# Attention kernel: chunks turned by VectorE from rows loaded by quarters, norms alone through TensorE

## The chip, the cores and the metric

The kernel runs on one core of one Trainium2 chip. A core has a matrix engine (TensorE, in the profile PE, with its weight loads PEld), a vector engine (VectorE, DVE), a scalar engine (ScalarE, ACT), GpSimd (POOL) and a sync engine (SyncE, SP) that here only issues DMAs. The engines run their own instruction streams in order and wait for each other by semaphores. SBUF holds 128 partitions; TensorE writes to PSUM, of which the kernel uses eight banks of 128x512 floats. The metric is the device time of one execution in microseconds, the median over several runs.

## The reference

The input `x` is four images of 32 channels and 128x128 pixels. A first layer unfolds each image into 128 channels (c, r1, r2) of 64x64 pixels and lets the rows of the folded image attend to each other; a second layer runs on the tokens.

```python
def _L0_conv_ref(x, gamma):
    xs = x.reshape(B, C, h, R, w, R).transpose(0, 1, 3, 5, 2, 4).reshape(B, C * R * R, h, w)
    q = xs.reshape(B, C * R * R, hw)
    energy = jnp.einsum('bci,bcj->bij', q, q)
    d = jnp.sqrt(jnp.diagonal(energy, axis1=1, axis2=2))
    energy = energy / (d[:, :, None] * d[:, None, :])
    attn = jax.nn.softmax(energy, axis=-1)
    out = jnp.einsum('bcj,bij->bci', q, attn).reshape(B, C * R * R, h, w)
    out = gamma * out + xs
    ...
# second layer, t = tokens of x
t = t + attention without softmax(layernorm(t))
t = t + two experts of eight, by a router(layernorm(t))
```

Here `hw` is 4096 pixels, so `energy` is 4096x4096 for each image: every pixel's vector of 128 channels against every other's, divided by both norms.

## The kernel before

Everything is in float32. The 4096 pixels of an image are eight chunks of `CH` = 512 (`NCH` = 8), each of four blocks of 128 (`NJ`). Two forms of each chunk are needed: `qT`, pixels on partitions (the values, and the right side of the sums), and `qn`, channels on partitions, each pixel divided by its norm (both sides of the energy).

`attend(b, st)` runs the first layer for image `b`. For chunk `i` and every chunk `jc` up to `i` it takes four steps; in each a product `pe` (L556), its exponential `pr` by ScalarE (L559, with the row sums), and two steps later a product `po` with `qT` (L440). As the matrix is symmetric, the part above the diagonal is made from the part below: VectorE turns 32x32 blocks of `pr` into `F` (L369, L513), SP writes `F` to DRAM as `blocks` and brings it back as `G` (L483, L491), and some `LAG` = 57 units of a work clock later TensorE multiplies it into `pg` (L375), which VectorE adds to `o` (L385). `o` holds a chunk's sums as channels by pixels; ScalarE copies the first part into it from `po` (L445).

The second layer of image `b` (`layer1`: `close_rows`, `matrix`, `attention_rows`, `sorted_experts`) is a generator that is moved on between the steps of `attend` from 84% of image `b` on, and runs into image `b + 1`. `close_rows` divides the rows: `rdx` (1 over the sum, spread), its transposes `pbd` (L722), four multiplies `df` (L709) from PSUM, and an add into `T` (L731), the image's tokens.

`prep(b, kc, st)` prepares the pair `kc` of chunks (`2 kc` and `2 kc + 1`) and is the subject here. It loads `xx`, 128 partitions of (s, r1, c) with eight rows each, by four DMAs of 128 KB (L279). Image 0 loads all its `xx` into the buffer of `T`; the others have one buffer of the pool `xin`. TensorE transposes it in two groups of four (`ptq`, L313) and VectorE copies them out into `qT` (L302). VectorE squares `qT` and sums (L324, L325) and GpSimd takes the power -1/2 (L164). VectorE scales `qT` into `qs` (L338), TensorE transposes `qs` in two groups of four (`ptn`, L346) and ScalarE copies them into `qn` (L344). The transposes' banks come from `hold`, which keeps a PSUM bank of `ps_t` (three) until its copy is issued.

Below, a list `timed` gives each `prep` its begin and end in percent of an image's work and a count of moves; each move takes two of its steps (`yield`). Chunk pairs 0 and 1 of the next image are prepared at 65 to 82% and 87 to 99% of an image, pairs 2 and 3 at 2 to 20% and 30 to 50% of the image itself. `input_rows` loads the tokens `T` (for image 0 as 32 DMAs of 64 KB, for the others as 16 of 128 KB). The order in which the instructions stand on PE, DVE, ACT and SP is the order in which these generators issue them (`manual_schedule`).

## Time and profile before

| | |
|---|---|
| median of 3 runs | 1708.52 us (1704.93 to 1710.81) |
| the profiled execution | 1712.1 us |
| its span | 1710.3 us |
| granted TensorE clock, mean | 0.994 |
| DMA | 355.25 MB, 208 GB/s over the span |
| first matmul starts, last ends | 5.7 us, 1702.3 us |

The profile is of one execution. Its page lists the busy time of each engine, then the span in 40 slices with the busy share in tenths. The groups collect instructions of one line, engine and operation: out<-in, the shape, the count, then the busy time and the mean ns of one, then the idle time of the engine just before them and what ended it. The timeline has the start, the duration, and engine, line and operation; an `x2` on a matmul of 128x512 is one product, which the engine makes in two passes. The windows give the same by stretches of time.

## The change

The prepared chunks are made in another way, and the pixels of a chunk stand in another order inside its blocks.

- `load_quarters` loads a pair of chunks as `xa`: partition (a, c) holds rows 4a to 4a + 3 of the pair's half images, in four DMAs of 128 KB with runs of 2 KB. `xa` has the tag `xx` of the one-buffer pool `xin`.
- `turn_quarters` makes `qT` from it by VectorE's 32x32 transposes, two of 128x256 for each chunk. The pixels in a partition of `qT` stand in an order that follows from the quarters; `in_order` and `in_turn` bring `o` and the products into one another.
- Only 1 over the norms goes through TensorE: VectorE spreads `rn` into `wide`, four transposes give `pnorm`, and four multiplies of 64x512 make `qn` from the rows `xx` and `pnorm`. The rows are loaded too: for image 0 they are its tokens `T`, loaded once at the same time as `xa`, for the others `xx`, into the buffer that `xa` has left, after the transposes.
- The load of `xa` is issued five steps before its first transpose (two for pair 1 of image 0).
- The first pair of image 0 has a function of its own, `prep_first`, with `xa`, with `qs` and `ptn` as before, and with 40 spare transposes (`keep_running`) where 22 were.
- The places in `timed` are others: pairs 0 and 1 at 52 to 78% and 80 to 99%, pairs 2 and 3 at 1 to 22% and 28 to 52%; `input_rows` runs for images 1 to 3 alone.

```diff
-    def prep(b, kc, st):
...
+    def chunks_of(b, kc, st):
+        qT = qpool.tile([P, 2, NJ, P], F32, tag="qT", name=f"qT_{b}_{kc}")
+        st.setdefault("qT", {})[2 * kc] = qT[:, 0]
+        st["qT"][2 * kc + 1] = qT[:, 1]
+        return qT
+    def channels(b, kc, s, st):
+        qn = npool.tile([P, CH], F32, tag="qn", name=f"qn_{b}_{2 * kc + s}")
+        st.setdefault("qn", {})[2 * kc + s] = qn
+        return qn
+    def squares(b, kc, s, qT, ss):
+        sq = work.tile([P, NJ, P], F32, tag="qs", name=f"sq_{b}_{kc}_{s}", bufs=2)
+        nc.vector.tensor_tensor(sq, qT[:, s], qT[:, s], ALU.mult)
+        nc.vector.tensor_reduce(ss[:, ts(s, NJ)], sq, AX.X, ALU.add)
+    def rows_of_image(b, kc, st):
+        rows = st["T"][:, ts(kc, 8), :]
+        return rows.rearrange("p k (w r) -> p k w r", r=2)
+    def load_quarters(b, kc, queues=(nc.sync, nc.sync)):
+        xa = xin.tile([P, 2, 2, 2, HW2, 2], F32, tag="xx", name=f"xa_{b}_{kc}")
+        halves = x[b].rearrange("c (s g) w -> c s (g w)", s=2)
+        for a in (0, 2, 1, 3):
+            first_row = 16 * kc + 4 * a
+            queues[a // 2].dma_start(
+                xa[ts(a, S)].rearrange("p s k r w e -> p s (k r w e)"),
+                halves[:, :, first_row * W : (first_row + 4) * W],
+            )
+        return xa
+    def turn_quarters(s, xa, qT):
+        for k in range(2):
+            nc.vector.transpose(
+                qT[:, s, 2 * k : 2 * k + 2, :].rearrange("p h (e r c) -> p r (h e) c", e=2, r=2),
+                xa[:, s, k].rearrange("p r (h t) e -> p (r h) e t", h=2),
+            )
+    def prep_first(st):
+        b, kc = 0, 0
+        st["T"] = big1.tile([P, KT, D], F32, tag="T", name="T_0")
+        xa = load_quarters(b, kc, (nc.sync, nc.scalar))
+        qT = chunks_of(b, kc, st)
+        yield
+        ss = stat.tile([P, 2 * NJ], F32, tag="ss", name=f"ss_{b}_{kc}")
+        rn = stat.tile([P, 2 * NJ, 1], F32, tag="rn", name=f"rn_{b}_{kc}")
+        for s in range(2):
+            turn_quarters(s, xa, qT)
+            squares(b, kc, s, qT, ss)
+            pow_neg_half(rn[:, ts(s, NJ), 0], ss[:, ts(s, NJ)])
+        keep_running(40, ps_g, "pg")
+        scaled = []
+        for s in range(2):
+            qs = work.tile([P, NJ, P], F32, tag="qs", name=f"qs_{b}_{kc}_{s}", bufs=2)
+            nc.vector.tensor_tensor(qs, qT[:, s], rn[:, ts(s, NJ)].to_broadcast([P, NJ, P]), ALU.mult)
+            scaled.append(qs)
+        for s, qs in enumerate(scaled):
+            qn = channels(b, kc, s, st)
+            pt, done = hold(f"ptn_{b}_{kc}_{s}", lambda p, qn=qn: nc.scalar.activation(qn, p, AF.Copy))
+            for j in range(NJ):
+                nc.tensor.transpose(pt[:, ts(j, P)], qs[:, j, :], ident)
+            done()
+            yield
+    def prep(b, kc, st):
+        ahead = 2 if b == 0 and kc == 1 else 5
+        xa = load_quarters(b, kc)
+        if b == 0:
+            load_tokens(st["T"][:, ts(kc, 8), :], b, 8 * kc, 8)
+            xx = rows_of_image(b, kc, st)
+        for _ in range(ahead):
+            yield
+        qT = chunks_of(b, kc, st)
+        for s in range(2):
+            turn_quarters(s, xa, qT)
+            yield
+        if b > 0:
+            xx = xin.tile([P, 8, HW2, 2], F32, tag="xx", name=f"xx_{b}_{kc}")
+            load_tokens(xx.rearrange("p k w r -> p k (w r)"), b, 8 * kc, 8)
+        ss = stat.tile([P, 2 * NJ], F32, tag="ss", name=f"ss_{b}_{kc}")
+        def scale(s, spread, view):
+            qn = channels(b, kc, s, st)
+            own = slice(s * 64, s * 64 + 64)
+            for r2 in range(2):
+                nc.vector.tensor_tensor(
+                    qn[ts(r2, 64)].rearrange("p (j a t) -> p a j t", a=4, t=S),
+                    xx[own].rearrange("p (a k) (h t) r -> p r a (k h) t", a=4, h=2)[:, r2],
+                    view(spread[own]),
+                    ALU.mult,
+                )
+        rn = stat.tile([P, 2 * NJ, 1], F32, tag="rn", name=f"rn_{b}_{kc}")
+        for s in range(2):
+            squares(b, kc, s, qT, ss)
+            if s == 1:
+                pow_neg_half(rn[:, :, 0], ss)
+            yield
+        for _ in range(ahead - 2):
+            yield
+        wide = work.tile([P, NJ, 2, 64], F32, tag="qs", name=f"wide_{b}_{kc}", bufs=2)
+        for s in range(2):
+            nc.vector.tensor_copy(wide[:, :, s], rn[:, ts(s, NJ)].to_broadcast([P, NJ, 64]))
+        yield
+        def scale_all(bank):
+            for s in range(2):
+                scale(s, bank, lambda ap: ap.rearrange("p (j a t) -> p a j t", a=4, t=S))
+        bank, done = hold(f"pnorm_{b}_{kc}", scale_all)
+        for j in range(NJ):
+            nc.tensor.transpose(bank[:, ts(j, P)], wide[:, j].rearrange("p s c -> p (s c)"), ident)
+        yield
+        done()
+        yield
@@ -367,6 +417,12 @@
         queued[:] = [q for q in queued if q[0] > tick[0]]
         for f in due:
             f()
+
+    def in_order(ap):
+        return ap.rearrange("p (a j c) -> p j a c", a=4, c=S)
+
+    def in_turn(ap):
+        return ap.rearrange("p (j a c) -> p j a c", a=4, c=S)
     def transposed_share(b, st, i, jc, G):
@@ -381,8 +437,7 @@
                 junk, G[:, :, ib], AF.Copy, accum_out=st["sums"][:, NJ * i + ib, jc : jc + 1]
             )
             if ib == NJ - 1:
-                o = st["o"][jc].rearrange("p (j a c) -> p a j c", a=4, c=S)
-                nc.vector.tensor_tensor(o, o, pg.rearrange("p (a j c) -> p a j c", a=4, c=S), ALU.add)
+                nc.vector.tensor_tensor(st["o"][jc], st["o"][jc], pg, ALU.add)
                 st["got"][jc] += 1
             yield "done" if ib == NJ - 1 else None
@@ -401,7 +456,7 @@
                     junk[:, :, : ib * S], rows, AF.Copy, accum_out=st["sums"][:, NJ * i + ib, NCH:]
                 )
             if step == (2, 1):
-                o = st["o"][i].rearrange("p (j a c) -> p a j c", a=4, c=S)[:, :, :3]
+                o = st["o"][i].rearrange("p (a j c) -> p a j c", a=4, c=S)[:, :, :3]
                 nc.vector.tensor_tensor(
                     o, o, pg[:, : 3 * P].rearrange("p (a j c) -> p a j c", a=4, c=S), ALU.add
                 )
@@ -442,7 +497,7 @@
                 )
                 if row["left"] == 0:
                     o = opool.tile([P, CH], F32, tag="o", name=f"o_{b}_{i}")
-                    nc.scalar.activation(o, row["po"], AF.Copy)
+                    nc.scalar.activation(in_order(o), in_turn(row["po"]), AF.Copy)
                     st["o"].append(o)
             def below(tiles, blks, i=i, values=values):
@@ -521,7 +576,8 @@
                     row["back"] = psum_t(f"back_{b}_{jc}")
                 nc.tensor.matmul(row["back"], qT[i][:, j, :], w, start=(j == 0), stop=(j == NJ - 1))
                 if j == NJ - 1:
-                    nc.vector.tensor_tensor(st["o"][jc], st["o"][jc], row["back"], ALU.add)
+                    o = in_order(st["o"][jc])
+                    nc.vector.tensor_tensor(o, o, in_turn(row["back"]), ALU.add)
                     st["got"][jc] += 1
                     banks[0] = 3
@@ -592,9 +648,8 @@
     def input_rows(b, st):
         st["T"] = T = big1.tile([P, KT, D], F32, tag="T", name=f"T_{b}")
-        nk = 4 if b == 0 else 8
-        for k in range(0, KT, nk):
-            load_tokens(T[:, k : k + nk, :], b, k, nk)
+        for k in range(0, KT, 8):
+            load_tokens(T[:, k : k + 8, :], b, k, 8)
             yield
             yield
             yield from idle(1)
@@ -707,9 +762,9 @@
                     for r2 in range(2):
                         rows = slice(r2 * 64, r2 * 64 + 64)
                         nc.vector.tensor_tensor(
-                            df[own, :, :, r2],
-                            o[rows].rearrange("p (k w) -> p k w", w=HW2),
-                            pb[own].rearrange("p (k w) -> p k w", w=HW2),
+                            df[own].rearrange("p (a k) (h t) r -> p r a (k h) t", a=4, h=2)[:, r2],
+                            o[rows].rearrange("p (a j t) -> p a j t", a=4, t=S),
+                            pb[own].rearrange("p (j a t) -> p a j t", a=4, t=S),
                             ALU.mult,
                         )
@@ -1318,29 +1373,29 @@
     steady = []
     UNITS = 3 * NJ * NJ * NCH * (NCH - 1) // 2 + 7 * NJ * NCH
-    first = prep(0, 0, states[0])
+    first, second = prep_first(states[0]), prep(0, 1, states[0])
     next(first)
     load_weights()
-    while 0 not in states[0].get("qn", {}):
-        next(first)
     next(first)
+    next(second)
+    load_tokens(states[0]["T"][:, 0:8, :], 0, 0, 8)
     ordered = ExitStack()
     ordered.enter_context(tc.manual_schedule(engines=ENGINES))
-    timed = [(first, 0, 1, 4)]
+    timed = [(first, 0, 1, 2), (second, 0.5, 5.5, 10)]
     for b in range(B):
         if b == 0:
-            for kc, begin, end in ((1, 0, 5), (2, 6, 20), (3, 25, 45)):
-                timed.append((prep(0, kc, states[0]), begin, end, 12))
+            for kc, begin, end in ((2, 6, 22), (3, 25, 48)):
+                timed.append((prep(0, kc, states[0]), begin, end, 16))
             timed.append((setup_weights(), 46, 58, 9))
             timed.append((setup_sorting(), 58, 98, 17))
         if b + 1 < B:
             nxt = states[b + 1]
-            timed.append((prep(b + 1, 0, nxt), 65, 82, 13))
-            timed.append((prep(b + 1, 1, nxt), 87, 99, 13))
-        begin, end, count = (52, 94, 17) if b == 0 else (36, 47, 9)
-        timed.append((input_rows(b, states[b]), begin, end, count))
+            timed.append((prep(b + 1, 0, nxt), 52, 78, 16))
+            timed.append((prep(b + 1, 1, nxt), 80, 99, 16))
+        if b > 0:
+            timed.append((input_rows(b, states[b]), 36, 47, 9))
         done = [0] * len(timed)
         start = clock[0]
         closing = None
@@ -1366,8 +1421,8 @@
                 pass
         timed = []
         if b + 1 < B:
-            timed.append((prep(b + 1, 2, nxt), 2, 20, 13))
-            timed.append((prep(b + 1, 3, nxt), 30, 50, 13))
+            timed.append((prep(b + 1, 2, nxt), 1, 22, 16))
+            timed.append((prep(b + 1, 3, nxt), 28, 52, 16))
     for steps, _ in steady:
         for _ in steps:
             pass
```

## What I predict

> **What bounds the kernel now.** I read the page first: busy shares, then the slices.

> ```profile
> PE 1651.3 (97%) x5458; PEld 875.0 (51%) x5458; DVE 934.7 (55%) x2443; ACT 925.2 (54%) x2893; POOL 512.0 (30%) x553
> ...
> PE   8999999999999999989999999999999999998897
> ...
> DVE  4433344467485345478478334547748533455686
> ```

> TensorE (PE) is the bound in every slice but the last few. VectorE (DVE) is about half busy, but has slices of 8 tenths (the digits at 470-513, 770-810 and 900-940 us). So a matmul taken out shortens the kernel by the time until the next one may start, unless a wait takes its place. Second, the groups by shape, for what the chunk preparation (`prep`, once per image `b` and pair of chunks `kc`, 16 in all) costs:

> ```profile
> L302 DVE COPY qT<-ptq 128x512 f32<-128x512 f32 x32 | 21.7, 679 | 33.1 <-PE ptq L313 26.7 <-PE pe L556 6.4
> L313 PE MATMUL ptq<-ident,xx 128*128 128x128 f32 x128 | 21.4, 294 | 10.8 <-DMA xx<-in_x_dram 7.1 <-issue 3.8
> L338 DVE TENSOR_TENSOR qs<-qT,rn 128x512 f32<-128x512 f32 x32 | 20.6, 682 | 1.5 <-POOL rn L164 1.5
> L346 PE MATMUL ptn<-ident,qs 128*128 128x128 f32 x128 | 19.5, 275 | 6.3 <-DVE o L385 3.1 <-issue 2.8 <-DVE qs L338 0.4
> L344 ACT ACTIVATE qn<-ptn 128x512 f32<-128x512 f32 x32 | 18.9, 590 | 16.3 <-PE ptn L346 16.1 <-issue 0.2
> L709 DVE TENSOR_TENSOR df<-o,pbd 64x512 f32<-64x512 f32 x64 | 43.9, 686 | 8.6 <-PE pe L556 3.9 <-PE pbd L722 3.5
> L369 DVE STREAM_TRANSPOSE F<-pr 128x512 f32<-128x512 f32 x440 | 306.0, 702 | 163.3 <-ACT pr L559 140.9 <-issue 14.8 <-DMA G<-blocks 5.5
> L513 DVE STREAM_TRANSPOSE F<-pr 128x128 f32<-128x128 f32 x186 | 44.0, 282 | 26.6 <-ACT pr L559 25.9 <-ACT junk L380 0.5 <-issue 0.2
> ```

> The mean of a matmul (294, 275 ns) holds its pipeline; what it takes from the stream is start to start. Third, therefore, the timeline, of PE and of the load queue (SP):

> ```profile
> 1361.07 0.60 PE L346 MATMUL ptn<-ident,qs 128*128 128x128 f32 x4
> 1361.50 0.59 PE L556 MATMUL pe<-qn,qn 128*128 128x512 f32 x1
> 1130.41 1.02 PE L375 MATMUL pg<-G,qT 128*128 128x512 f32 x2
> 1135.20 1.10 PE L313 MATMUL ptq<-ident,xx 128*128 128x128 f32 x4 [3.77 <-issue]
> 1121.65 10.25 SPq L279 DMA_DIRECT2D xx<-in_x_dram  x4
> 749.73 0.66 PE L346 MATMUL ptn<-ident,qs 128*128 128x128 f32 x4 [2.77 <-issue]
> ```

> Four `ptn` transposes take 0.43 us of the stream; four of `ptq` took 0.47 (1329.19 to 1329.66). Two of the lines show PE standing: 1135.20 because SP needed 10.25 us to issue four loads, 749.73 because `qs` stood in DVE's queue behind four `df`. Fourth, the stretches around such stalls (columns: span, PE, PEld, DVE, ACT, POOL busy, granted PE clock, DMA share, GB/s):

> ```profile
> 384.00:410.00 26.00, 26.00 (x94) 14.91 (x94) 23.29 (x56) 15.15 (x50) 1.94 (x3) 1.00 0.53 169
> 470.00:513.00 43.00, 42.36 (x135) 21.96 (x134) 36.73 (x139) 29.62 (x90) 11.83 (x15) 1.00 0.66 195
> 738.00:752.00 14.00, 11.14 (x33) 4.92 (x32) 13.65 (x32) 4.81 (x16) 8.32 (x7) 1.00 0.84 241
> 1130.00:1135.00 5.00, 1.43 (x4) 0.36 (x2) 0.00 (x0) 1.05 (x4) 3.28 (x4) 0.92 0.98 210
> 1135.00:1142.00 7.00, 6.80 (x15) 3.48 (x16) 3.13 (x7) 1.30 (x4) 1.91 (x2) 0.57 1.01 276
> 1160.00:1165.00 5.00, 4.29 (x9) 2.02 (x10) 4.79 (x19) 1.79 (x5) 2.49 (x3) 0.66 1.04 319
> ```

> The clock column matters: after the stalls at 1130 and 1160 it is 0.57 and 0.66, so such a stall costs more than its own length.

> **The change, part by part.**

> *PE work.* Each of the 15 pairs after the first loses two groups of `ptq` and two of `ptn` and gains one of `pnorm` (four 128x128 transposes, like `ptn`): 2 x 0.47 + 2 x 0.43 - 0.43 = 1.37 us; 15 x 1.37 = **-20.6 us**. Nothing hides this; PE is the bound wherever they stand.

> *Stalls that stood on the removed groups.* From start-to-start times, PE waited over 0.9 us on `ptq` or `ptn` four times: 727.0 (1.5), 749.7 (2.9), 1135.2 (3.9), 1160.7 (3.2), 11.6 us in all, always at pair 1 of images 2 and 3. After two of them the clock was down: 5 x 0.08 + 7 x 0.43 + 5 x 0.34 = 5.1 us. Both causes move: `ptq` is gone, and pair 1 starts at 80% of an image instead of 87%, so that in the order of the changed kernel its `pnorm` stands before the first `pbd` and its `df`. **-16.7 us.**

> *DVE.* Per pair it loses two copies (0.679) and two `qs` (0.682), 2.72 us, and gains four transposes of 128x256, two broadcasts `wide` (128x256, like `rdx`, 0.375) and four multiplies of 64x512 with a PSUM operand. A 128x256 transpose lies between 0.282 and 0.702; I take 0.42. It reads with a step of two elements, which no transpose of the trace does, so at the far end twice that; but `df` writes with that step and takes 0.686, as much as contiguous adds (0.685), so 0.42 stands. The multiplies have the form of `df`: 4 x 0.69. Sum 1.68 + 0.75 + 2.76 - 2.72 = +2.47 us, 15 times 37 us: 935 becomes 972, 57%. ACT loses 30 copies of 0.59, 18 us. The other layout of `o` I cost at nothing: the add of L385 already walks `o` in blocks of 32 at 685 ns, the one of L524 goes straight at 684.

> *Where that lateness lands.* `pnorm` waits for `wide`, on PE's stream, with `pe`, `po` and `pg` of the next steps behind it. Two places are full. Pair 2 (from 1% of the image) now has its squares, `wide` and multiplies among the last two `close_rows` of the previous image: the order has 64x512 `df` eight times there, and 384-410 is already busy 23.29 of 26. From `pg` of the preceding step to `pnorm` PE has about 2.6 us of work, DVE an add (0.55) and `wide` (0.75): one us of slack. Price: the 2.9 us of 749.7, up to 3.9; plus a third of a clock drop (3.4 us lost at full, by 7 x 0.43 + 0.4), so 3.5, three images: 10.5. Pair 3 (from 28%) lands in the routing and sorting, 36.73 of 43 plus my 7.9; there about 7.7 us of PE work stand between the last transpose ahead of `wide` and `pnorm`, so most lag is absorbed: 1 each, 3. Together **+13.5**; bounds 0 and 6 x 6.9 (the stall of 1135 with its clock drop) = 41.

> *Loads.* Images 1 to 3 read their pairs twice: 12 x 0.5 MB, 48 more issues on SP, ahead of `blocks` and `G`; image 0 drops 32 issues of T and gains 16. A quarter load is 64 runs of 2 KB against 256 of 512 bytes. `xx` shares its one buffer with `xa`, so SP waits for the last transpose of `xa`; behind it stand `blocks<-F` and `G<-blocks`, which `pg` needs 57 clock units later (14.7 us). 0.5 MB at the 270 GB/s of the full stretches is 1.9 us; it can bite at pair 1 alone: between 0 and 3 x 6.9, I take **+2**.

> *Start.* Before, the first `pe` starts at 13.62. Now: quarters landed at about 4.5 (between 3 and the 5.7 of before), three transposes, square, reduce to 7.7, power 1.0, `qs` 0.69, `ptn` and its copy: 11.1. But `pnorm` of pair 1 stands behind the second step of row 1, and its chain (four transposes, two squares and reduces 2.7, power 1.66, `wide`) ends at about 21.2, so the third step of row 1 starts at 21.65, before 21.14; row 1 then saves its two `ptn` groups. Against the 1.37 already counted: **+1**, between -2.5 and +4. The 40 spare transposes (22 took 4.41) end before `qs`.

> Sum: -20.6 - 16.7 + 13.5 + 2 + 1 = **-20.8**. The profiled execution took 1712.1 (span 1710.3), 3.6 over the median of 1708.5; taken off the median: **1688**.

> [...] The rows make TensorE transposes the dear ones here, because it is their engine that is full. [...]

> **Rivals.**
> 1. *Nothing takes the stalls' place*: DVE's lag stays inside the six `pr` buffers and `wide` is early. For it: no `ptn` of pairs 0, 2 and 3 waited over 0.6 us before. Against: `wide` of pair 2 is queued behind fuller work. 1708.5 - 20.6 - 16.7 + 1 = 1672.
> 2. *The quarters come late*: the load at 80% meets full DMA (0.98 at 1130), DVE stands on it in order, then PE, at pair 1 of three images, 6.9 each: 1687.7 - 2 + 20.7 = 1706, no change. Against: a quarter of the runs.
> 3. *Slower: DVE's queue decides.* `pnorm` waits at pairs 2 and 3 of images 1 to 3, each 6.9 us: 1687.7 - 13.5 + 41.4 = 1716. It decides from 5.7 us per place ((20.8 + 13.5) / 6); a transpose at 0.84 would add 1.7 us to each chain.
> 4. *The change not doing what it says* can hardly be: the order has 15 `pnorm` groups and no `ptq`.

> **Numbers.** Forecast 0.52 (own range 1680-1696), rival 1 0.22, rival 2 0.14, rival 3 0.12. Three runs spread by 0.3%, so 0.3% (5.1 us) is what can be told. Faster: 0.52 + 0.22 + a third of rival 2 = 0.78; same 0.11; slower 0.11. Range 1674 to 1706: it leaves out rival 3 and the lower part of rival 1.

> **What would show it.** PE count 5458 - 128 - 120 + 60 + 18 = 5288; DVE near 972, ACT near 907; no PE stall at pair 1; stalls of PE in front of `pnorm` at the image starts, with the clock below 1.00 there; DVE near full in 470-513. Wrong if the quarter transposes take 0.8, if `G<-blocks` starts to hold `pg`, or if PE stalls where no `pnorm` stands.

## The result, and the profile after

The changed kernel took 1728.65 us (median of 7 runs, 1724.07 to 1733.28) and the kernel before, measured beside it, 1710.84 us (7 runs, 1704.93 to 1720.04): every run of the changed kernel was slower than every run of the one before. The ratio is 1.0089, 95% interval 1.0068 to 1.0111. The forecast was 1688 us, with a range of 1674 to 1706: it was wrong in sign and size. Three lines of the changed kernel's page, the busy shares and two rows of the slices:

```profile
PE 1647.2 (95%) x5288; PEld 859.7 (50%) x5288; DVE 964.1 (56%) x2535; ACT 907.9 (53%) x2863; POOL 510.6 (30%) x553
...
PE   8999999999999999899998999989999999998898
...
DVE  5443343665693444569377354556758433454686
```

PE has 170 instructions fewer, as forecast. Between its two ends, its row of slices had one 8 before (727 to 770 us); now it has three, at 692 to 735, 908 to 951 and 1124 to 1167 us. The groups by shape, with what ended the idle time before them:

```profile
L316 DVE STREAM_TRANSPOSE qT<-xa 128x256 f32<-128x256 f32 x64 | 23.5, 412 | 15.3 <-PE po L495 8.3 <-DMA xa<-in_x_dram 7.1
L372 DVE TENSOR_TENSOR qn<-xx,pnorm 64x512 f32<-64x512 f32 x48 | 32.8, 683 | 7.9 <-PE pnorm L397 7.3
L388 DVE COPY wide<-rn 128x256 f32<-128x256 f32 x30 | 7.2, 280 | 1.1 <-POOL rn L164 1.1
L397 PE MATMUL pnorm<-ident,wide 128*128 128x128 f32 x60 | 9.2, 276 | 8.0 <-DVE wide L388 8.0
```

The new operations cost what was forecast or less (0.412 for 0.42, 0.683 for 0.69, 0.280 for 0.375), and the read with a step of two costs nothing that shows (between 0.282 at 128 elements and 0.702 at 512, a straight line gives 0.42 at 256). So the loss is in waits. Taken from start to start of the matmuls, with the median distance between starts for each width as its nominal cost, PE's own work fell from 1616.6 to 1597.9 us; what it lost between matmuls rose from 81.7 to 123.5. The view of waits (engine and line waiting, what ended it: us in total, times, longest) says at what:

```profile
DVE o L460 <- remote: 28.3, 3, 9.5
ACT pr L615 <- remote: 27.1, 5, 7.1
PE pe L612 <- ACT pr L615: 18.4, 13, 3.6
PE pg L431 <- DMA G<-blocks: 10.8, 5, 4.0
PE pnorm L397 <- DVE wide L388: 8.0, 4, 2.5
```

The same view of before:

```profile
ACT pr L559 <- remote: 12.1, 3, 5.5
PE pe L556 <- ACT pr L559: 6.0, 7, 3.1
PE pg L375 <- DMA G<-blocks: 4.1, 2, 2.3
```

"remote" is a wait whose end the profile can tie to no instruction that had just ended. The timeline of all engines shows one, in the middle of image 1:

```profile
548.07 0.82 PE L451 MATMUL pg<-G,qT 128*128 128x256 f32 x4
...
552.16 1.02 PE L431 MATMUL pg<-G,qT 128*128 128x512 f32 x2
...
555.94 0.56 DVE L460 TENSOR_TENSOR o<-o,pg 128x384 f32<-128x384 f32 x1 [9.46 <-remote]
555.99 0.60 ACT L615 ACTIVATE pr<-pe 128x512 f32<-128x512 f32 x1 [5.62 <-remote]
...
556.73 2.07 PE L612 MATMUL pe<-qn,qn 128*128 128x512 f32 x2 [3.54 <-ACT pr L615]
```

VectorE's add needs the four passes of `pg` that start from 548.07 to 548.62, and it starts at 555.94. In the trace the last update of PE's semaphore is at 548.82 and the next six come at 555.92 to 556.13, 0.04 us apart: the completions of six products arrived together, up to 7 us late. ScalarE, VectorE and GpSimd stood, then PE, and the stretch behind it ran at half clock, 0.51 from 556 to 563 (columns: span, busy PE, PEld, DVE, ACT, POOL, granted clock, DMA share, GB/s):

```profile
553.00:556.00 3.00, 0.18 (x1) 0.00 (x0) 0.06 (x1) 0.01 (x1) 0.32 (x1) 1.00 0.08 26
556.00:563.00 7.00, 6.27 (x8) 2.64 (x9) 3.02 (x5) 3.16 (x10) 3.83 (x4) 0.51 0.69 224
```

The same comes at 973 and 1387 us, in images 2 and 3.

## The experiments

Two theories stood at the start: the loss comes from where the preparations stand (PLACES), or from the loads read twice (LOADS); a third was that `pnorm` on VectorE's queue sets it off (QUEUE). The first four kernels ran beside each other on one chip, where before took 1704.12.

*Places of before.*

```diff
-  pairs 0, 1, 2, 3 at 52-78, 80-99, 1-22, 28-52, 16 moves each
+  pairs 0, 1, 2, 3 at 65-82, 87-99, 2-20, 30-50, 13 moves each
```

> The changed kernel, with its preparations at the places of before: pair 0 at 65 to 82% of an image, pair 1 at 87 to 99, pair 2 at 2 to 20, pair 3 at 30 to 50, 13 steps each; all else as changed. Three theories. PLACES: the 42 us that PE lost between matmuls more than before come from where the steps stand (pair 3 in the densest part of the routing, its loads packed in half the window): then the 2.0 us waits at pnorm of pair 3 and the 3.5 us stand at about 48% of an image go, and the time falls by 12 to 28, to 1701 to 1717. LOADS: they come from the second load of the rows and the four quarter loads, whose number does not change here: 1725 to 1732, with the stands moved along. QUEUE: pnorm waits on VectorE wherever it stands: 1722 to 1732, with waits of 1 to 3 us at pnorm in each image.

1697.64 us, 0.9953 (0.9934 to 0.9971).

*Spread over the windows.*

```diff
-  timed.append((prep(b + 1, 3, nxt), 28, 52, 16))   # and 0, 1, 2
+  timed.append((prep(b + 1, 3, nxt), 28, 52, 8))
```

> The changed kernel, with 8 instead of 16 moves for each preparation of images 1 to 3 in the same windows, so that its 15 steps fill the whole window and not its first half; the last loads and the norms come later. PLACES: the crowding goes, and with it part of the stands: 1708 to 1722. LOADS: the same bytes lie further apart, so the stands in front of pg at pair 1 (4.2 and 3.5 us) shrink but the one at 48% stays: 1718 to 1728. QUEUE: unchanged within 4, 1724 to 1732, as pnorm still follows wide by one step, unless a step falls clear of the routing (then pair 3 gains its 2.0 us and the clock drop of 1.7, 11 in all: 1718).

1682.86 us, 0.9874 (0.9855 to 0.9893). PE's stands over 0.9 us in front of `pnorm` fell from 8.6 us to 2.6, which is the one at the start.

*The broadcast earlier.*

```diff
+  slack = min(2, ahead - 2)
-  for _ in range(ahead - 2):        # then wide, then one yield
+  for _ in range(ahead - 2 - slack): # then wide, then 1 + slack yields
```

> The changed kernel, with the broadcast wide two half-steps earlier in each preparation from pair 2 of image 0 on, so that TensorE has two more half-steps of work between the last work of VectorE that pnorm needs and pnorm. QUEUE: the 2.0 us waits at pnorm of pair 3 go, with their clock drops: 3 x (2.0 + up to 1.7) = 6 to 11 off, 1718 to 1723, and if those waits also set off the stand at 48% by upsetting the order of arrivals, 20 to 26 off, 1703 to 1709. LOADS and PLACES: the pnorm waits go but the stand at 48% (3.5 us and a clock drop, each of three images) and the waits for G at pair 1 stay: 1718 to 1723.

1689.19 us, 0.9913 (0.9895 to 0.9930). The 2.0 us waits in front of `pnorm` of pair 3 are gone; 1.1 us each are left at the next matmul that waits for VectorE (`pcnt`, of the sorting).

*Rows not loaded again.*

```diff
-  xx = xin.tile([P, 8, HW2, 2], F32, tag="xx", ...)
-  load_tokens(xx..., b, 8 * kc, 8)
+  xx = qT.rearrange("p s j (w r) -> p (s j) w r", r=2)
```

> The changed kernel without the second load of each pair of images 1 to 3: the four multiplies that scale the channels read the chunk qT in its place, so the channels of these images hold other values than the reference's; every instruction of the engines but the 48 issues and their 6.3 MB is there. LOADS: the waits for G at pair 1 (4.2 and 3.5 us, 6.8 us at half clock after the first) and the stands at 48% (3 x 3.5 and their clock drops) go: 15 to 28 off, 1701 to 1714. PLACES and QUEUE: off at most the 3 us by which xa may be let go earlier: 1724 to 1731.

1694.91 us, 0.9933 (0.9909 to 0.9956), with `pg` still standing 2.9 us at 733 and 2.2 at 1136.

All four were faster than before, and none of the four profiles has a single wait of the kind at 555.94 ("remote", over 1.5 us; called a late wait below, and the completion that it waits for a late one). All four also lie below every range that the three theories had given, which were set against the 1728.65 us of the first result. So these four decide none of the theories, and the changed kernel itself had to be measured again beside the next ones.

*The two kernels as they are.* No edit.

> The changed kernel as it is, once more, beside the others of this call. In its first profile PE's completions reached VectorE and ScalarE up to 7 us late at 549, 966 and 1380 us, and each of the four variants already run showed none of that and was faster than before. Theory OWN: the lateness belongs to the program (its order of steps brings the transfers, the scatter and the diagonal share together), so it is there again at the same three places, and the ratio to before is again 1.007 to 1.011 (1716 to 1723 where before takes 1704). Theory OCCASION: it belongs to the occasion on which that profile was taken and the four variants were only lucky in it; then it is absent or elsewhere, and the time is 1700 to 1708, ratio 0.998 to 1.003, with the 2.0 us waits at pnorm and the waits for G still there.

1727.34 us, 1.0083 (1.0058 to 1.0108), with 10 late waits in its profile, at 556 and 1383 the same 9.5 us of VectorE.

> The kernel before as it is, for a profile beside the others. OWN: its stands are those of the first profile (3.9 us in front of ptq at 1135, 2.9 and 3.2 in front of ptn at 750 and 1161, 3.2 in front of pe at 770), 1702 to 1712. OCCASION: the stands that followed late completions (770) are gone, those that followed a late load or VectorE's queue stay: 1700 to 1706.

1711.02 us, 7 late waits.

*Later shares.*

```diff
-  LAG = 57     # and 16 moves each
+  LAG = 65     # and 8 moves each
```

> Preparations spread over their windows as in e2_spread, and the shares pg taken 65 instead of 57 units of the clock after their G was asked for (2 us more). What is left of waits in e2_spread is in front of pg for G at pair 1 (3.4 us at 725, 2.2 at 1111, 2.6 at 1138, half clock after them). If the loads of pair 1 only delay G by about 3 us, these waits go: 10 to 14 off e2_spread, ratio 0.979 to 0.982 (1669 to 1673 where before takes 1704). If instead G waits for a buffer or the queue, later shares free the three buffers later and nothing is won: ratio 0.986 to 0.991.

1724.96 us, 1.0062 (1.0040 to 1.0084): nothing won, and outside both ranges. It holds two edits, and spreading all four with 57 units did not run on this chip, so which of the two lost is open.

*Pair 3 alone spread.*

```diff
-  timed.append((prep(b + 1, 3, nxt), 28, 52, 16))
+  timed.append((prep(b + 1, 3, nxt), 28, 52, 8))
```

> The changed kernel, with pair 3 of images 1 to 3 alone spread over its window of 28 to 52% (8 instead of 16 moves). If what the change lost all hangs on pair 3 meeting the routing (the waits at pnorm, and the late completions behind them), this alone gives most of what spreading all four pairs gave: ratio 0.989 to 0.993 (1685 to 1692 where before takes 1704). If the crowding of pairs 0 to 2 and their loads counts as much, a third of it at most: 1.000 to 1.005.

1701.48 us, 0.9925 (0.9902 to 0.9948). With one number changed it takes 26 us less than the changed kernel on the same chip. The waits of that kernel (c1_changed_again):

```profile
ACT pr L615 <- remote: 19.9, 3, 7.0
DVE o L460 <- remote: 18.9, 2, 9.5
PE pe L612 <- ACT pr L615: 15.2, 11, 3.6
PE pnorm L397 <- DVE wide L388: 8.0, 4, 2.5
```

and of the one with pair 3 spread:

```profile
ACT pr L615 <- remote: 14.3, 4, 6.7
PE pe L612 <- ACT pr L615: 6.8, 8, 3.0
PE pnorm L397 <- DVE wide L388: 2.4, 1, 2.4
```

Completions come late in both (10 waits each), but PE stands less than half as long behind them, the one at VectorE's diagonal add (`o` L460) is gone, and so is `pnorm` of pair 3.

*Without indirect transfers.* Each of the late waits so far (55 in six profiles; the text below has 45, without those of e6) ended 0.8 to 3.6 us after the start of one of GpSimd's indirect transfers; 36 to 37% of the span lies so close behind one. The next pair takes those transfers out.

```diff
-  nc.gpsimd.indirect_dma_start(xs[h], offset(place...), xn[:, k, :], None)
+  nc.gpsimd.dma_start(xs[h][ts(n, P), :], xn[:, k, :])
-  nc.gpsimd.indirect_dma_start(yb[...], None, ys, offset(place...))
+  nc.gpsimd.dma_start(yb[...], ys[ts(n, P), :])
```

> The kernel before, with GpSimd's 384 indirect transfers (scatter of tokens to the experts, gather of the results) replaced by transfers of the same tiles to and from fixed rows: tokens meet the wrong experts, so the output is not the reference's; matmuls, VectorE, ScalarE and the bytes stay. Late completions of PE (a semaphore of PE that VectorE or ScalarE sees 2 to 9 us after the matmul) lay, in the six profiles that have any, without exception in the stretches in which indirect transfers run, 38% of the span (45 of 45). Theory INDIRECT: the indirect transfers hold the completions up; without them no wait of this kind is left and the stands behind them go: 5 to 12 off, ratio 0.993 to 0.997. Theory FULL: the full transfers in those stretches do it, whoever asks for them: ratio 0.998 to 1.002, late completions still there.

1704.65 us, 0.9983 (0.9967 to 0.9998): in the range of FULL, but with none late.

> The changed kernel with the same replacement. What decides is its ratio against e7_plain_before. LATE (the late completions turned the gain into a loss): without them the change keeps its gain of work, less the waits at pnorm and for G: the ratio of the two is 0.988 to 0.998. WAITS (the change's own new waits, at pnorm and in front of pg at pair 1, are enough for the loss): the ratio of the two stays 1.005 to 1.011.

1692.87 us, 0.9927 (0.9902 to 0.9951); against e7_plain_before 0.9927 / 0.9983 = 0.9944.

> The changed kernel as it is, beside the others of this call. In the four profiles of e1 to e4 no completion came late, in the others (the two kernels and e5, e6) some did in every one. OWN: 1.006 to 1.011 of before wherever it runs. OCCASION: where no completion comes late in its profile, the ratio is 0.994 to 1.002; where some do, 1.006 to 1.011.

1696.54 us, 0.9943 (0.9925 to 0.9961), no late wait. So the replacement moved nothing that can be told from the noise (0.9944 and 0.9943): this chip shows no late completion with the indirect transfers either, and e7 and e8 can't tell INDIRECT from FULL.

> All four preparations spread over their windows, as in e2_spread, beside the changed kernel itself. If spreading them is worth what it seemed (0.9874 there, without late completions): 0.985 to 0.990 again. If what it won was the absence of late completions, and it gives much back where they occur, as e5_spread_lag65 did (1.0062): 1.000 to 1.007.

1684.66 us, 0.9880 (0.9860 to 0.9900).

Two more sets of three, with the kernels as above and no further edit; they ran on a chip that shows no late completion either:

> The changed kernel as it is, as the measure for the two beside it. Where completions of PE come late in its profile: 1.006 to 1.011 of before, as twice so far; where none does: 0.993 to 0.996, as in c3_changed_third.

1695.89 us, 0.9953 (0.9932 to 0.9974), none late.

> The changed kernel with the 384 indirect transfers replaced by transfers of the same tiles to and from fixed rows (tokens meet the wrong experts), as in e8_plain_changed. It tells something only where c4_changed_fourth shows late completions. INDIRECT (they are held up by the indirect transfers): none late here, and 0.990 to 0.997 of before while c4 is at 1.006 to 1.011. FULL (any full transfers do it): late completions here too, and within 0.003 of c4. Where c4 shows none, 0.991 to 0.996 by both.

1690.93 us, 0.9915 (0.9884 to 0.9945).

> All four preparations spread over their windows, as in e2_spread and e9_spread_again (0.987 and 0.988 without late completions). Where c4_changed_fourth shows late completions: if pair 3 meeting the routing is what makes them costly (theory of e6_spread_pair3, 0.9925 there), 0.985 to 0.995; if any order loses to them, 1.000 to 1.008. Where c4 shows none: 0.986 to 0.990.

1682.50 us, 0.9861 (0.9829 to 0.9892).

> The kernel before as it is, for its profile beside the two others. Either it shows late completions of PE, as in both its profiles so far (5 and 7 waits of over 1.5 us behind them): then the two kernels beside it can tell what holds the completions up. Or it shows none, and is the first profile of before to compare the undisturbed profile of the changed kernel with (c3_changed_third, span 1692.6): then the stands at pair 1 (726, 749, 1131, 1156: 1.4 to 3.2 us) are there and the one in front of pe at 769 is not, span 1700 to 1705.

1700.32 us (one run), span 1698.5, none late: the undisturbed profile of before. Its stands at pair 1 are there, the one in front of `pe` at 769 is not.

> As f1_plain_again. Where the profile of before beside it shows late completions: INDIRECT 0.990 to 0.997 of before and none late; FULL 1.004 to 1.011 and some late. Where it shows none: 0.991 to 0.996 by both.

1696.02 us, 0.9957 (0.9942 to 0.9972).

> As f2_spread_third. Where the profile of before beside it shows late completions: 0.985 to 0.995 if pair 3 meeting the routing is what makes them costly, 1.000 to 1.008 if any order loses to them. Where it shows none: 0.986 to 0.990.

1679.22 us, 0.9855 (0.9837 to 0.9873), just below its range.

What the sets say together:

| chip | late waits in the profiles | before, us | changed to before |
|---|---|---|---|
| of the first result (not named) | before 5, changed 14 | 1710.84 | 1.0089 |
| 8 | before 7, changed 10, e5 9, e6 10 | 1714.29 | 1.0083 |
| 7 | none in 4 | 1704.12 | not run |
| 5 | none in 4 | 1707.27 | 0.9943 |
| 6 | none in 6 | 1703.22, 1703.35 | 0.9953 |

So OWN and OCCASION were both half right: the lateness does not belong to one kernel, and where it comes the changed kernel pays more for it. All profiles of one chip agree, but each chip was used on one occasion only (chip 6 twice within minutes), so whether it comes with the chip or with the occasion is not shown. The changed kernel is faster by 0.5% on two chips and slower by 0.8 to 0.9% in the two other measurements.

## Why the prediction was wrong

The undisturbed profiles, those without late completions (before: span 1698.5; changed: 1692.6 and 1689.6), give 6 to 9 us less, and the ratios 8 to 10 us, where -20.8 was forecast. So some 11 to 15 us of the miss are steps of the sum that were wrong; the rest, 24 to 28 us and the sign with it, shows only where completions come late, for which the sum had no term. By the steps of the sum:

- *PE work, -20.6*: right. PE's own work went from 1616.6 to between 1596.8 and 1597.9 us in the changed kernel's profiles, -18.7 to -19.8. What the rows said, that a TensorE transpose is dear where that engine is full (PE at 97%), held for its own work.
- *Removed stalls, -16.7*: **this step failed.** "Both causes move" was wrong: `ptq` is gone, but PE now stands at the next matmul that waits for a transfer. Without late completions, the waits of before (5.7 of `ptq` is the wait for the first load of all):

```profile
PE ptq L313 <- DMA xx<-in_x_dram: 10.6, 4, 5.7
PE ptn L346 <- DVE qs L338: 6.5, 3, 3.1
PE pg L375 <- DMA G<-blocks: 4.9, 3, 2.6
```

and of the changed kernel (c3_changed_third):

```profile
PE pg L431 <- DMA G<-blocks: 9.1, 3, 3.9
PE pnorm L397 <- DVE wide L388: 8.0, 4, 2.5
PE ptn L344 <- DVE qs L338: 1.0, 1, 1.0
```

The timeline shows one such place, in image 1. First before, PE with the issues of SP around it:

```profile
711.66 1.74 SPq L491 DMA_DIRECT2D G<-blocks  x4
713.92 9.95 SPq L279 DMA_DIRECT2D xx<-in_x_dram  x4
725.90 1.84 SPq L491 DMA_DIRECT2D G<-blocks  x4
726.44 0.72 PE L313 MATMUL ptq<-ident,xx 128*128 128x128 f32 x4 [1.57 <-DMA xx<-in_x_dram]
734.53 1.10 PE L375 MATMUL pg<-G,qT 128*128 128x512 f32 x2
```

and the changed kernel:

```profile
694.87 1.88 SPq L546 DMA_DIRECT2D G<-blocks  x4
698.31 3.88 SPq L279 DMA_DIRECT2D xx<-in_x_dram  x4
708.82 2.98 SPq L546 DMA_DIRECT2D G<-blocks  x4
712.99 1.02 PE L495 MATMUL po<-pr,qT 128*128 128x512 f32 x2
717.33 1.60 PE L431 MATMUL pg<-G,qT 128*128 128x512 f32 x2 [3.32 <-DMA G<-blocks]
718.72 1.92 PE L612 MATMUL pe<-qn,qn 128*128 128x512 f32 x2
```

In both kernels a load stands in SP's queue between two groups of `G`, which are then issued 14.2 and 14.0 us apart instead of 10.3 (701.39 to 711.66 before). Before, PE was held up by `ptq` and came to the first `pg` of the late `G` at 734.34; the last part of that `G` landed at 734.44. Nothing holds the changed kernel up earlier, and it stands 3.3 us in front of `pg`, with slower matmuls behind it (the two passes of `pe` at 718.72 take 1.92 us, those of `po` at 712.99 took 1.02). It is not the new place of pair 1: e1_old_places has the old one and stands there too (3.4 us at 730, 3.5 at 1137). Nor is the second load needed for it: without it, in e4_rows_once, four stores `out_dram` take the queue for 9.57 us at 714 and `pg` still stands 2.9 us.

Stands over 0.9 us on `ptq` and `ptn` fell from 12.4 us to 1.2 to 1.3, and those on `pg` rose from 4.6 to 13.0 and 14.0. The stands of this term were worth about -2 instead of -11.6, and the 5.1 us of clock that it took off with them did not go (below). The prediction's last lines named this ("if `G<-blocks` starts to hold `pg`") without giving it a price.
- *DVE's lateness, +13.5*: right in kind, the places were not. (Its own working, 2.9 plus a third of 3.4, is 4.0 a place, not 3.5.) Pair 2 has no stand in front of `pnorm` (3 x 3.5 forecast); pair 3 has 2.0 us in each of three images (3 x 1 forecast), in every profile of the changed kernel. Measured 6. e3_wide_early took these away and came to 0.9913, against 0.9943 and 0.9953 on other chips: 5 to 7 us, with intervals that all but touch.
- *Loads, +2*: not shown either way. Without the second load the ratio was 0.9933, against 0.9943 and 0.9953 on other chips; that is 2 to 3 us, but inside the intervals. Whether the quarter loads hold `G` up at pair 1, or the full stretch by itself, was not tried.
- *Start, +1*: right in two of four profiles. The 21st `pe` (at 28.7 us before) comes 1.2 and 1.4 us later in the undisturbed profiles, where the clock halved at 21.5, behind the first `pnorm`; in the two others it did not, and they are 0.3 us earlier.

With what was measured, and the load at its forecast: -19 - 2 + 6 + 2 + 1 = -12, against -6 to -10. Most of the rest is the clock: until the last matmul the undisturbed profile of before has four periods of 3.41 us at half clock, those of the changed kernel seven each, up to 5.1 us more.

**No term at all stood for the completions that come late.** Between matmuls PE loses 69.9 us in the undisturbed profile of before and 80.7 and 81.7 in the two others; in the changed kernel 84.2 and 87.8 against 116.9 and 123.5. So where completions come late, before loses some 11 us more and the changed kernel some 29 to 39, and that turns its gain into a loss. The part that can be followed in the traces: the stands over 0.9 us in front of `pe`, of which the undisturbed profiles have none, are 2.4 and 3.2 us in before and 15.5 and 18.5 in the changed kernel, and half clock takes up to 18.8 us from the changed kernel (eleven periods of 3.41 us in the first profile) instead of 11.9 (seven). The remainder, which may hold other differences between the chips, was not taken apart. The profile before had the sign, 12.1 us of `pr` waiting for "remote", and the 3.2 us stand in front of `pe` at 770; the prediction does not speak of them.

Why the changed kernel pays more is shown in part. Sixteen moves of two steps end the 15 steps of pair 3 in half of its window; e6_spread_pair3, which halves this pace and nothing else, has as many late waits and runs 26 us faster on that chip. Not all of the 26 us belongs to late completions: spreading all four pairs also won 12 and 13 us on the chips without them (e9 against c3, f2 against c4). And the pace is not the whole of it: e5_spread_lag65 has the slow pace too, and lost. How the pace makes late completions dearer (the adds of VectorE, the two loads in half the time) was not taken apart.

Of the rivals, the third (slower, 1716, VectorE's queue) had the side of the result and the region, not the mechanism: its 6.9 us in front of `pnorm` never came, the dear stands were in front of `pe`; that it named the right side is luck. The second (1706, a ratio of 0.9985: pair 1's stretch stays full) is somewhat nearer to the undisturbed 0.9943 and 0.9953 than the forecast (0.988), at another instruction than it named. The first, that nothing takes the stalls' place, is out.

On the clock: behind the stand of 3.2 us at 1160 of before it was 0.50 from 1161.51 to 1164.92, and in the changed kernel of equal stands of 2.0 us at `pnorm` of pair 3 the one at 510.6 in the first profile had a drop behind it, the one at 510.0 in c3_changed_third had none. In the two profiles of the first result, of before and of the changed kernel, all changes of the granted clock between the first and the last matmul lie whole multiples of 3.41 us apart, and its periods at 0.50 last 3.41 or 6.83 us. Cut along this grid, the first profile of the changed kernel has the stand in one window, and the next window runs at half clock (columns as above):

```profile
508.28:511.69 3.41, 1.55 (x10) 1.14 (x10) 3.31 (x10) 0.03 (x1) 2.50 (x4) 1.00 1.04 301
511.69:515.10 3.41, 3.41 (x5) 1.33 (x4) 3.16 (x13) 1.19 (x4) 2.50 (x4) 0.50 0.95 230
```

In c3_changed_third an edge, at 509.58 (143 windows after the halving at 21.5), cuts the stand in two, and the clock stays at 1.00:

```profile
506.16:509.58 3.42, 2.02 (x5) 0.57 (x3) 3.21 (x14) 1.30 (x4) 2.50 (x4) 1.00 1.00 344
509.58:512.99 3.41, 2.96 (x14) 1.98 (x15) 3.17 (x13) 1.17 (x4) 2.74 (x3) 1.00 1.06 289
512.99:516.40 3.41, 3.41 (x13) 1.90 (x12) 3.37 (x8) 1.60 (x8) 2.55 (x3) 1.00 0.95 285
```

Spreading the four preparations (0.9855 to 0.9880 in four measurements on three chips) beats both kernels where no completion comes late, by 1.2 to 1.5% against before. Where they do, pair 3 spread alone does (0.9925, one measurement); all four with 57 units were not tried there.

## What to carry to other kernels

A stall that ends with a transfer landing in a full stretch need not go with the instruction that stood there (here the stands on `ptq` and `ptn` fell by 11 us and those on `pg` rose by 8 to 9): look which instruction waits next for the same queue, and price it there. It pays to try whether work that is spread by a pace fills its window: halving the pace of one of four preparations was worth 26 us here where completions came late, more than the matmuls saved. And a profile is of one chip on one occasion: the same kernel took 0.9943 and 1.0083 of the time of the same other one, so a change of under 1% wants more than one chip before it is called.

## What was not expected of the hardware

In six of the twenty profiles completions of TensorE reached the other engines late, some of them in a burst: 55 waits of over 1.5 us (14 in the first profile of the changed kernel, the longest 9.5), none in the fourteen others, with the same or nearly the same programs. Three of them, in the first profile of the changed kernel, are alike to 0.05 us: VectorE is idle for 9.46, 9.47 and 9.42 us up to 555.9, 973.4 and 1387.4, and the six held updates come 1.4 to 1.7 us after the last packet of a run of transfers, one of the indirect transfers' queue, has ended (554.31 to 555.92, 971.65 to 973.34, 1385.96 to 1387.34). Other bursts came while transfers ran on (at 936.5 and 1366.5). All 55 end within 3.6 us of the start of an indirect transfer; whether these are the cause stays open, since the kernels without them ran only where none came late.
